# Two attention layers on one core: more split steps in the second layer, sums and outputs added by transfers, projections in half blocks

## The chip, the cores and the metric

The kernel runs on one core of a Trainium2 chip. The metric is the time of one execution on the device in microseconds. The engines are named as in the profile: PE is TensorE (PEld its weight loads), DVE is VectorE, ACT is ScalarE, POOL is GpSimd, SP issues most transfers.

## The reference

Two self-attention layers follow each other on x of 4 images with 4096 tokens of 256 channels, all in float32. Query and key have 32 channels; the second layer's values have 128.

```python
# layer 0
q, k, v = x @ Wq + bq, x @ Wk + bk, x @ Wv + bv          # 32, 32, 256 channels
attn = softmax(einsum('bnd,bmd->bnm', q, k), axis=-1)    # 4096 x 4096 per image
x = gamma * einsum('bnm,bmc->bnc', attn, v) + x
# layer 1
f, g, v = x @ Wf + bf, x @ Wg + bg, x @ Wh + bh          # 32, 32, 128 channels
beta = softmax(einsum('bqd,bkd->bqk', g, f), axis=-1)
x = x + einsum('bqk,bkd->bqd', beta, v) @ Wo + bo
```

## The kernel before

`fast_path` does all the work; `general_path` runs only when a flag, worked out at the end, says that values were out of range. The order is image by image, and in an image first layer, then second layer. A layer is cut into blocks of queries (first layer 16 blocks of 256, second layer 8 blocks of 512), and a block into **steps** over keys: 8 steps of 512 keys in the first layer, 16 steps of 256 keys in the second. There are 1024 steps in all, 128 for a layer of an image.

A step (`class Step`) has these parts:

- `scores`: TensorE multiplies keys and queries into the one score buffer `st` (128 x 1024, `ps_st` has one buffer), and ScalarE takes the exponential into `p`. The scores of step n + 2 are issued in the loop's turn for step n.
- In a **split** step the exponential is also taken with a small negative bias into `high`, rounded to the fast float32r form; VectorE makes `low` = p - high (`cut_low`) and `d` from low and high (`cut_both`). The values have three such parts too. The product is then three fast products (high, low and d, each with its part of the values), not one float32 product. All first-layer steps are split; in the second layer those with `i % 5 == 2`, three of 16 (2, 7, 12).
- `products_first`, `products_second`: TensorE adds the products into accumulators in PSUM. A whole second-layer step makes two float32 products of 512 columns, each two instructions in the profile; a split one makes six single ones.
- In the second layer VectorE also adds every step's p into `p_sum` (a copy for the first step, L696, then additions, L698), for the softmax's denominators.

Tiles come from pools with tags; tiles of one tag share its buffers, and a new one waits until an old one has been read. `wide` gives p three buffers (tag p), and high and p of a second-layer split step two (tag t); low and d share two (tag l).

After a block, `end_first` forms the new x: it writes it to DRAM (`x1_dram`), and x plus the second layer's bias to another DRAM tile (`x1_res`). `end_second` joins two accumulators and sums p_sum; its four output units multiply by Wo (L624), make the denominators (L625), and VectorE forms the result from PSUM and the reloaded x1_res (`load_old`, L605, L628), which SP writes to `out`.

Projections (`project_units`) of a block of 512 tokens are units too: transpose and split into parts, query and key projection with a store to DRAM (`qk_dram`), and values. POOL loads queries and keys back from DRAM, row by row (`load_q`, `load_k`). The next image's first-layer projections run beside this image's second layer, one block of tokens beside each block of queries; the second layer's run beside the first, the last of them in the second layer's first block. In image 0, three blocks are projected ahead of the first step, the other five within the first block.

The units are issued in the loop, after the scores of a later step and ahead of the step's products, paced evenly over the block's steps:

```python
        pace = NI[l] - (5 if l == 1 else 1)
        upto = min(len(units), -(-len(units) * (s.i + 1) // pace))
        todo = units[done:upto]
```

The Tile framework plans the final order of the instructions on each engine from this program order, with its own view of costs, and sets all waits. So an engine's order in the trace can differ from the written one; once planned it is fixed.

Of the kernel before, what the change touches and what calls it, by code (L numbers as in the profile page):

```python
# [61 lines left out]
EPS = 2.0**-12  # L63
AHEAD = 3

# [168 lines left out]
def fast_path(ctx: ExitStack, tc: tile.TileContext, x, w0, w1, wo, bo, gamma, out, off):  # L234
# [13 lines left out]
    split = [[l == 0 or i % 5 == 2 for i in range(NI[l])] for l in range(2)]  # L248
# [11 lines left out]
    def wide(tag, name, dtype=F32):  # L260
        return work.tile([P, 2 * QB], dtype, tag=tag, bufs={"d": 1, "p": 3}.get(tag, 2), name=name)
# [5 lines left out]
    def load_squares(key, tokens):  # L267

        turned[key] = []
        for c in range(NCC):  # L270
            t = work.tile([P, QB], F32, tag="squares", bufs=5, name=f"squares_{key[0]}_{key[1]}_{key[2]}_{c}")
            for a in range(P // S):
                ch = c * P + a * S
                nc.sync.dma_start(
                    t[a * S : (a + 1) * S, :].rearrange("j (b i) -> j b i", i=S),
                    tokens[:, ch : ch + S].rearrange("(b j) i -> j b i", j=S),
                )
            turned[key].append(t)

    def load_block(b, j):  # L280
        if b < B and j < NB:
            load_squares((b, 0, j), x[b, j * QB : (j + 1) * QB, :])


    x_nat = {}

    def load_first(j):
        if j < NB:
            x_nat[j] = []
            for n in range(j * NT, (j + 1) * NT):  # L290
                x_nat[j].append(data.tile([P, C], F32, tag="v1", bufs=V1, name=f"x_nat_{n}"))
                nc.sync.dma_start(x_nat[j][-1], x[0, n * P : (n + 1) * P, :])

    load_first(0)
    load_first(1)
# [8 lines left out]
    seen_v = const.tile([P, 2, B * NB, 2], F32, name="seen_v")  # L304
# [61 lines left out]
    xT, x_parts, k_t, v_t = {}, {}, {}, {}  # L366
    qk_dram, x1_dram, x1_res = {}, {}, {}
    q_t = {}


    def transpose_unit(b, l, j):
        def issue():
            xT[b, l, j] = data.tile([P, NCC, QB], F32, tag="xT", name=f"xT_{b}_{l}_{j}")
            for c in range(NCC):
                if b == l == 0:
                    ps = side_psum(f"psx_{j}_{c}")
                    for t in range(NT):
                        nc.tensor.transpose(ps[:, t * P : (t + 1) * P], x_nat[j][t][:, c * P : (c + 1) * P], ident)
                    nc.scalar.copy(xT[b, l, j][:, c, :], ps)
                else:  # L380
                    nc.vector.transpose(xT[b, l, j][:, c, :], turned[b, l, j][c])
            x_parts[b, l, j] = []
            for c in range(NCC):
                parts = [
                    work.tile([P, QB], F32R, tag="squares", bufs=5, name=f"x{what}_{b}_{l}_{j}_{c}") for what in "hl"
                ]
                nc.scalar.copy(parts[0], xT[b, l, j][:, c, :])  # L387
                nc.vector.tensor_sub(parts[1], xT[b, l, j][:, c, :], parts[0].bitcast(F32))  # L388
                x_parts[b, l, j].append(parts)
            if b == l == 0:  # L390
                load_first(j + 2)
            elif l == 0:
                load_block(b, j + 1)
            elif j == NB - 1:
                load_block(b + 1, 0)

        return issue

    def split_values(v, h, low, d, seen):
        nc.scalar.activation(h, v, AF.Copy, scale=1.0 - DOWN)  # L400
        nc.scalar.activation(low, v, AF.Abs, accum_out=seen)
        nc.vector.scalar_tensor_tensor(d, h.bitcast(F32), -1.0 - EPS, v, ALU.mult, ALU.add)
        nc.vector.scalar_tensor_tensor(low, d.bitcast(F32), 1.0 / EPS, h.bitcast(F32), ALU.mult, ALU.add)

    def project_units(b, l, j):
        key = (b, l, j)

        def qk_unit():
            ps = side_psum(f"psqk_{b}_{l}_{j}")
            for c in range(NCC):  # L410
                for n in range(2):
                    nc.tensor.matmul(  # L412
                        ps,
                        wqk[l][:, c, :],
                        x_parts[key][c][n],
                        start=(c == n == 0),
                        stop=(c == NCC - 1 and n == 1),
                    )
            whole = data.tile([2 * D, QB], F32, tag="qk", name=f"qk_{b}_{l}_{j}")
            parts = data.tile([P, QB], F32R, tag="qk_parts", name=f"qk_parts_{b}_{l}_{j}")  # L420
# [6 lines left out]
            qk_dram[key] = dram.tile([2, 2, D, QB], F32, name=f"qk_dram_{b}_{l}_{j}")  # L427
            nc.sync.dma_start(qk_dram[key].rearrange("h w d n -> (h w d) n"), parts.bitcast(F32))
            if b == l == 0:
                near = parts.rearrange("(h w d) n -> h w d n", h=2, w=2)  # L430
                load_k(b, l, j, near)
                if j == 0:
                    load_q(b, l, j, near)

        per = QB // CV[l]

        def v_unit(t0):
            def issue():
                ps = side_psum(f"psv_{b}_{l}_{j}_{t0}").rearrange("p (t c) -> p t c", c=CV[l])
                for t in range(per):  # L440
                    for c in range(NCC):
                        nc.tensor.matmul(  # L442
                            ps[:, t, :],
                            xT[key][:, c, (t0 + t) * P : (t0 + t + 1) * P],
                            wv[l][:, c, :],
                            start=(c == 0),
                            stop=(c == NCC - 1),
                        )
                tiles = slice(t0, t0 + per)
                seen = [seen_v[:, l, b * NB + j, n : n + 1] for n in range(2)]  # L450
                if l == 0:
                    split_values(ps, *(v0[j][what][:, tiles, :C] for what in ("h", "l", "d")), seen[t0 // per])
                    return
                for n in range(NT // G[1]):
                    i = j * NT // G[1] + n
                    v = ps[:, n * G[1] : (n + 1) * G[1], :]
                    if split[1][i]:
                        t = data.tile([P, 3, G[1], P], F32R, tag="v1_parts", bufs=sum(split[1]), name=f"v_{b}_{i}")
                        v_t[b, i] = {what: t[:, m] for m, what in enumerate(("h", "l", "d"))}
                        split_values(v, *v_t[b, i].values(), seen[n])  # L460
                    else:
                        v_t[b, i] = data.tile([P, G[1], P], F32, tag="v1", bufs=V1, name=f"v_{b}_{i}")
                        nc.scalar.copy(v_t[b, i], v)
                        nc.scalar.activation(v, v, AF.Abs, accum_out=seen[n])  # L464

            return issue

        return [transpose_unit(b, l, j), qk_unit] + [v_unit(t0) for t0 in range(0, NT, per)]

    def load_rows(dst, parts, which, halves):  # L470
        for n, h in enumerate(halves):
            nc.gpsimd.dma_start(dst[n * D : (n + 1) * D, :], parts[h, which])  # L472

    def load_q(b, l, j, parts=None):
        q_t[b, l, j] = data.tile([P, QB], F32R, tag="q", bufs=2, name=f"q_{b}_{l}_{j}")
        load_rows(q_t[b, l, j], qk_dram[b, l, j].bitcast(F32R) if parts is None else parts, 0, (0, 0, 1, 1))

    def load_k(b, l, j, parts=None):
        k_t[b, l, j] = data.tile([P, QB], F32R, tag="k", bufs=NB, name=f"k_{b}_{l}_{j}")
        load_rows(k_t[b, l, j], qk_dram[b, l, j].bitcast(F32R) if parts is None else parts, 1, (0, 1, 0, 1))  # L480
# [8 lines left out]
    class Step:  # L489
# [8 lines left out]
        def scores(self):  # L498
# [18 lines left out]
            nc.scalar.activation(self.p, s_flat, AF.Exp)  # L517

# [5 lines left out]
        def cut_both(self):  # L524
            if self.split:
                self.d = wide("d" if self.l == 0 else "l", f"d_{self.key}", F32R)
                nc.vector.scalar_tensor_tensor(  # L527
                    self.d, self.low.bitcast(F32), -1.0 / EPS, self.high.bitcast(F32), ALU.mult, ALU.add
                )

# [13 lines left out]
        def products_second(self, acc):  # L544
            v = v_t[self.b, self.i]
            some = [i for i in range(NI[1]) if split[1][i]]
            for p, v, which, first, last in (
                (
                    (self.high, v["h"], 0, self.i == some[0], False),
                    (self.low, v["l"], 0, False, self.i == some[-1]),  # L550
                    (self.d, v["d"], 1, self.first, self.last),
                )
                if self.split
                else ((self.p, v, 1, self.first, self.last),)
            ):
                for g in range(G[1]):
                    nc.tensor.matmul(  # L557
                        acc[which],
                        v[:, g, :],
# [6 lines left out]
    def end_first(b, j, acc):  # L566
# [11 lines left out]
        def residual(s):  # L578
            def issue():
# [6 lines left out]
                if part == 0 and s == 0:  # L586
                    x1_dram[b, jj] = dram.tile([QB, C], F32, name=f"x1_dram_{b}_{jj}")
                    x1_res[b, jj] = dram.tile([QB, C], F32, name=f"x1_res_{b}_{jj}")
# [53 lines left out]
    for j in range(AHEAD):  # L642
        run(project_units(0, 0, j))
# [153 lines left out]
```

## Time and profile before

| what | value |
|---|---|
| time, median of 3 runs (lowest, highest) | 3222.8 us (3222.76, 3225.62) |
| the profiled execution's own time | 3222.18 us |
| its span, first to last instruction | 3220.4 us |
| granted TensorE clock | 0.998 |
| PE, DVE, ACT, POOL busy | 3166.5, 2691.5, 1988.8, 661.3 us |
| DMA engines, hardware queue and software queue | 16.0%, 4.5% |
| first layer of image 0, 1, 2, 3 | 488.9, 451.9, 451.9, 451.9 us |
| second layer of image 0, 1, 2, 3 | 341.8, 343.5, 343.5, 322.7 us |

A row of the profile's groups gives the line, the engine, the operation, the tiles (out<-in), the shapes and the count, then busy time and the mean of one in ns, then the idle time of the engine ahead of these instructions and what ended it. The stage times are from the starts of the first score matmul (L505) of each stage in the timeline; the first image's first layer starts 24.2 us into the span, and the last figure goes to the end of the span.

### The profile page before, as it was taken

How to read it: one execution, taken by the hardware profiler on the slowest of the kernel's cores; microseconds unless marked ns; L12 is line 12 of the kernel's file. 1: busy time of each engine (PE TensorE's matmuls, PEld its weight loads, DVE VectorE, ACT ScalarE, POOL GpSimd, SP SyncE). 2: the span in 40 equal slices, each digit the busy share in tenths (PEclk: the TensorE clock that was granted, in tenths of full speed). 3: DMA queues.
4: the chain of work that ended last, by engine and by line, in shares of the span. 5: the costliest groups of instructions: out<-in, count | busy, mean ns of one | idle time of the engine just before them, and what ended most of it. 6: DMA issues, size and time to landing. Idle time of an engine off the chain costs nothing. (4 is left out here: it accounts for less than half of the span.)

```text
span 3220.4 us, 51144 instructions
## 1 busy us (share of the span) xinstructions
PE 3166.5 (98%) x19460; PEld 2613.0 (81%) x19460; DVE 2691.5 (84%) x3181; ACT 1988.8 (62%) x2483; POOL 661.3 (21%) x784
## 2 busy tenths in 40 slices
PE   8999999999999999999999999999999999999998
PEld 7999997566799999655679999966558999995554
DVE  7888888888888888788888888878888888887776
ACT  6666666655566666565556666655555666665554
POOL 3222223000232222200022222310002222241000
PEclk9999999999999999999999999999999999999999
DMA  4111123221212112322121112232222211121110
GB/s 120 47 47 44 50 50 83 56 53 49 59 44 54 44 52 49 79 53 53 49 64 42 49 50 50 61 70 52 51 52 57 53 41 47 46 70 47 36 36 31
DMA packets 368653, 172.16 MB, mean 53 GB/s; under 512 B 257392, under 2 KB 343664, under 8 KB 368400
## 3 DMA queue, kind: packets, MB, share of 16 engines
q1 hardware_dynamic: 342528, 134.29, 16.0%
q0 software_dynamic: 24960, 34.18, 4.5%
q8 instruction: 157, 2.57, 0.3%
q14 instruction: 96, 0.79, 0.1%
q10 hardware_dynamic: 912, 0.33, 0.0%
HBM read 99.22 MB, written 67.11 MB: 52 GB/s over the span
## 5 line engine op out<-in xcount | busy, mean ns | idle before, releaser
L517 ACT ACTIVATE p<-st 128x1024 f32<-128x1024 f32 x1024 | 1044.5, 1020 | 393.6 <-PE st L505 369.5
L515 ACT ACTIVATE high<-st,down 128x1024 fp32r<-128x1024 f32 x608 | 678.8, 1116 | 683.6 <-PE st L505 572.7
L527 DVE SCALAR_TENSOR_TENSOR d<-low,high 128x1024 fp32r<-128x1024 f32 x608 | 761.2, 1252 | 208.3 <-PE acc L536 202.9
L522 DVE TENSOR_TENSOR low<-p,high 128x1024 fp32r<-128x1024 f32 x608 | 810.6, 1333 | 134.2 <-ACT p L517 134.2
L557 PE MATMUL acc<-p,v 128*128 128x512 f32 x1664 | 795.2, 597 | 0.0
L505 PE MATMUL st<-q,k 128*128 128x256 f32 (+1 forms) x3072 | 778.6, 361 | 8.4 <-ACT p L517 8.3
L698 DVE TENSOR_TENSOR p_sum<-p_sum,p 128x1024 f32<-128x1024 f32 x480 | 587.1, 1223 | 60.7 <-ACT p L517 47.5
L505 PEld LDWEIGHTS st<-q,k 128*128 128x128 f32 x3072 | 461.2, 189 | 210.7 <-ACT p L517 113.3
L536 PE MATMUL acc<-v0d,d 128*128 128x258 f32 x4096 | 591.7, 284 | 1.7 <-DVE d L527 1.6
L536 PE MATMUL acc<-v0h,high 128*128 128x258 f32 x4096 | 588.6, 283 | 1.6 <-ACT high L515 1.6
L536 PE MATMUL acc<-v0l,low 128*128 128x258 f32 x4096 | 587.0, 283 | 0.5 <-DVE low L522 0.5
L536 PEld LDWEIGHTS acc<-v0d,d 128*128 128x128 f32 x4096 | 533.1, 189 | 6.7 <-DVE d L527 3.6
L536 PEld LDWEIGHTS acc<-v0h,high 128*128 128x128 f32 x4096 | 534.1, 190 | 3.4 <-ACT high L515 2.0
L536 PEld LDWEIGHTS acc<-v0l,low 128*128 128x128 f32 x4096 | 532.7, 189 | 0.8 <-DVE low L522 0.7
L557 PEld LDWEIGHTS acc<-p,v 128*128 128x128 f32 x1664 | 308.4, 190 | 214.3 <-issue 184.7
L593 POOL TENSOR_TENSOR x_res<-x,bo 128x256 f32<-128x256 f32 x128 | 216.3, 1690 | 889.9 <-DVE g L583 482.0
L472 POOL DMA_DIRECT2D q<-qk_dram x252 | 123.9, 501 | 1166.1 <-PE st L505 1143.0
L676 POOL TENSOR_TENSOR x_res<-x_res,bv 128x256 f32<-128x256 f32 x128 | 189.6, 1482 | 114.4 <-DMA x_res<-in_x 85.0
L442 PE MATMUL psv<-wv,xT 128*128 128x128 f32 (+1 forms) x1024 | 194.8, 331 | 6.8 <-DVE qk L423 6.1
L442 PEld LDWEIGHTS psv<-wv,xT 128*128 128x128 f32 x1024 | 159.6, 192 | 29.8 <-DVE qk L423 8.5
L472 POOL DMA_DIRECT2D k<-qk_dram x224 | 109.6, 500 | 245.2 <-PE st L505 140.3
L388 DVE TENSOR_TENSOR xl<-xT,xh 128x512 fp32r<-128x512 f32 x128 | 87.1, 683 | 5.1 <-ACT xh L387 4.7
(96 smaller groups left out, 1701.9 us busy)
## 6 DMA issues: line engine op xcount, KB each, us to landing
x_res<-in_x SPq DMA_DIRECT2D x128, 128.0 KB, 2.2
qk_dram<-qk_parts SPq DMA_DIRECT2D x64, 256.0 KB, 2.1
x_dram<-x SPq DMA_DIRECT2D x128, 128.0 KB, 1.7
x_res<-x_res SPq DMA_DIRECT2D x128, 128.0 KB, 1.7
squares<-x_dram SPq DMA_DIRECT2D x256, 64.0 KB, 2.3
x_old<-x_res SPq DMA_DIRECT2D x128, 128.0 KB, 2.0
out<-x_old SPq DMA_DIRECT2D x128, 128.0 KB, 1.7
q<-qk_dram POOLq DMA_DIRECT2D x252, 64.0 KB, 2.1
```

The costliest lines, as they stand in the source:

```text
L442: nc.tensor.matmul(ps[:, t, :], xT[key][:, c, (t0 + t) * P : (t0 + t + 1) * P], wv[l][:, c, :], start=(c == 0), stop=(c == NCC - 1),)
L472: nc.gpsimd.dma_start(dst[n * D : (n + 1) * D, :], parts[h, which])
L505: nc.tensor.matmul(st[:, g, :], k_t[b, l, kt // NT][:, kt % NT * P : (kt % NT + 1) * P], q_t[b, l, j * n // QB][:, q0 : q0 + n], start=Tru ...
L515: nc.scalar.activation(self.high, s_flat, AF.Exp, bias=down)
L517: nc.scalar.activation(self.p, s_flat, AF.Exp)
L522: nc.vector.tensor_sub(self.low, self.p, self.high.bitcast(F32))
L527: nc.vector.scalar_tensor_tensor(self.d, self.low.bitcast(F32), -1.0 / EPS, self.high.bitcast(F32), ALU.mult, ALU.add)
L536: nc.tensor.matmul(acc[2 * s + which][:, :W], p[:, g * QB0 + s * P : g * QB0 + (s + 1) * P], v0[self.i][v][:, g, :], start=self.first and ...
L557: nc.tensor.matmul(acc[which], v[:, g, :], p[:, g * QB : (g + 1) * QB], start=first and g == 0, stop=last and g == G[1] - 1,)
L593: nc.gpsimd.tensor_add(x_old[s], x_new[s], bo_sb)
L676: nc.gpsimd.tensor_add(x_res[b, j][t], x_res[b, j][t], bv)
L698: nc.vector.tensor_add(p_sum, p_sum, s.p)
```

## The change

There are four parts.

- The second layer's split steps are six of 16 (`SPLIT1`) instead of three.
- The exponentials of five of the whole steps (`MOVED_SUMS`) are not added by VectorE: POOL's queue copies the first into an SBUF tile (tag e, one buffer) and adds the other four to it with accumulating transfers. VectorE starts its own sum by adding the first two that remain, and `end_second` adds the moved sum.
- `end_first` writes x plus bias straight to `out`. The output unit scales its product on ScalarE into `y`, and POOL's queue adds y to `out` with an accumulating transfer. `x1_res` and `load_old` are gone.
- Projections are done in half blocks of 256 tokens, at steps named in a `plan`: the transpose, two steps (four in the first layer) later the query and key projection, one step later the values. In the second layer a half of the next image's starts every seven steps. In image 0's lead, odd halves use the buffers of tag v1_parts, so that two halves are under way. Square loads (transposing reads) are issued by half, when the half before has been projected.

The core of the diff:

```diff
+SPLIT1 = (1, 4, 6, 9, 11, 14)
+MOVED_SUMS = (0, 3, 7, 10, 13)
...
-    split = [[l == 0 or i % 5 == 2 for i in range(NI[l])] for l in range(2)]
+    NH = N // QB0
+    split = [[l == 0 or i in SPLIT1 for i in range(NI[l])] for l in range(2)]
...
             nc.scalar.activation(self.p, s_flat, AF.Exp)
+            if l == 1 and i in MOVED_SUMS:
+                if i == MOVED_SUMS[0]:
+                    moved_sums[b, j] = wide("e", f"p_sum_moved_{b}_{j}")
+                    nc.gpsimd.dma_start(moved_sums[b, j], self.p)
+                else:
+                    nc.gpsimd.dma_start(moved_sums[b, j], self.p, accum_op=ALU.add)
...
+        def add_up(self, p_sum):
+            if self.l == 0 or self.i in MOVED_SUMS:
+                return
+            kept = [i for i in range(NI[1]) if i not in MOVED_SUMS]
+            if self.i == kept[0]:
+                first_p.append(self.p)
+            elif self.i == kept[1]:
+                nc.vector.tensor_add(p_sum, first_p.pop(0), self.p)
+            else:
+                nc.vector.tensor_add(p_sum, p_sum, self.p)
...
-                nc.sync.dma_start(x1_res[b, jj][row : row + P, :], x_old[s])
+                nc.sync.dma_start(out[b, n * P - b * N : (n + 1) * P - b * N, :], x_old[s])
...
+        nc.vector.tensor_add(p_sum, p_sum, moved_sums[b, j])
         nc.vector.tensor_add(sums, p_sum[:, :QB], p_sum[:, QB:])
...
-                nc.vector.scalar_tensor_tensor(y[t], ps[:, :C], inverse[:, 1, n : n + 1], y[t], ALU.mult, ALU.add)
+                y = small(f"y_{key}_{t}")
+                nc.scalar.activation(y, ps[:, :C], AF.Copy, scale=inverse[:, 1, n : n + 1])
                 row = j * QB + t * P
-                nc.sync.dma_start(out[b, row : row + P, :], y[t])
+                nc.gpsimd.dma_start(out[b, row : row + P, :], y, accum_op=ALU.add)
...
+    lead = [project_units(0, 0, h) for h in range(2 * AHEAD)]
+    run([u[0] for u in lead[:2]])
+    for h in range(2 * AHEAD):
+        run(lead[h][1:])
+        run([u[0] for u in lead[h + 2 : h + 3]])
...
+    def plan(b, l, j, ends):
+        units = {}
+        def put(i, *some):
+            units.setdefault(i, []).extend(some)
+        if l == 0:
+            if j >= 2:
+                t, qk, v = project_units(b, 1, j - 2)
+                put(0, t), put(4, qk), put(5, v)
+            for n, u in enumerate(ends):
+                put(1 + n, u)
+            return units
+        if j == 0:
+            for n, u in enumerate(ends):
+                put(1 + n, u)
+            for n, h in enumerate((NH - 2, NH - 1)):
+                t, qk, v = project_units(b, 1, h)
+                put(6 * n, t), put(6 * n + 2, qk), put(6 * n + 3, v)
+        else:
+            for n, u in enumerate(ends):
+                put(1 + n, u)
+        if b + 1 < B:
+            for h in range(NH):
+                i = 12 + 7 * h - j * NI[1]
+                for n, u in zip((0, 2, 3), project_units(b + 1, 0, h)):
+                    if 0 <= i + n < NI[1]:
+                        put(i + n, u)
+        return units
```

The transpose unit for a half now makes one transpose and one pair of parts for both halves of the channels (128 x 512), as large as one of the two of a block before; the query and key projection has 256 columns instead of 512; a value unit has the same size as before in the first layer.

## The prediction

> **What bounds the kernel now.** I read the page first: engine shares, then the costliest groups, then the timeline of TensorE to find where each block of queries begins, last the waits and the timeline of ScalarE inside one block.
>
> ```profile
> PE 3166.5 (98%) x19460; PEld 2613.0 (81%) x19460; DVE 2691.5 (84%) x3181; ACT 1988.8 (62%) x2483; POOL 661.3 (21%) x784
> ...
> L517 ACT ACTIVATE p<-st 128x1024 f32<-128x1024 f32 x1024 | 1044.5, 1020 | 393.6 <-PE st L505 369.5
> L515 ACT ACTIVATE high<-st,down 128x1024 fp32r<-128x1024 f32 x608 | 678.8, 1116 | 683.6 <-PE st L505 572.7
> L527 DVE SCALAR_TENSOR_TENSOR d<-low,high 128x1024 fp32r<-128x1024 f32 x608 | 761.2, 1252 | 208.3 <-PE acc L536 202.9
> L522 DVE TENSOR_TENSOR low<-p,high 128x1024 fp32r<-128x1024 f32 x608 | 810.6, 1333 | 134.2 <-ACT p L517 134.2
> L557 PE MATMUL acc<-p,v 128*128 128x512 f32 x1664 | 795.2, 597 | 0.0
> ...
> L698 DVE TENSOR_TENSOR p_sum<-p_sum,p 128x1024 f32<-128x1024 f32 x480 | 587.1, 1223 | 60.7 <-ACT p L517 47.5
> ```
>
> TensorE is busy 98%, VectorE 84%. A matmul's mean (597 ns on L557) includes its pipeline; what counts is the spacing of issues in the timeline. There I read 0.43 us for each of the four instructions of a whole second-layer step, 0.215 us for one of the six in a split step and for a score matmul of 512 columns, 0.12 us for 256 or 258 columns. So a whole step costs TensorE 4 x 0.43 + 2 x 0.215 = 2.15 us, a split step 6 x 0.215 + 0.43 = 1.73, a first-layer step 24 x 0.12 + 4 x 0.12 = 3.35.
>
> The starts of the score matmuls give the stages. First-layer blocks take 27.0 without and 29.6 us with a projection, against 8 x 3.35 = 26.8 and 29.4 of issue: nothing to win. Second-layer blocks 2 to 7 of images 0 to 2 take 41.75 us (block 1: 40.4), the first block 52.6; in the last image, which projects nothing ahead, 37.2 and 45.0. Issue per block: 13 x 2.15 + 3 x 1.73 = 33.1, outputs 4 x 0.66 = 2.6, projection 20 x 0.215 = 4.3: 40.1 or, without projection, 35.8. So **1.4 to 1.7 us of each block is idle, and near 8 to 10 of the first**. The chain of exponentials shows how the idle time arises:
>
> ```profile
> 3021.11 1.11 ACT L515 ACTIVATE high<-st,down 128x1024 fp32r<-128x1024 f32 x1 [1.17 <-PE st L505]
> 3022.12 1.02 ACT L517 ACTIVATE p<-st 128x1024 f32<-128x1024 f32 x1
> 3023.94 1.02 ACT L517 ACTIVATE p<-st 128x1024 f32<-128x1024 f32 x1 [0.81 <-PE st L505]
> 3026.13 1.02 ACT L517 ACTIVATE p<-st 128x1024 f32<-128x1024 f32 x1 [1.16 <-PE st L505]
> ```
>
> There is one score buffer (ps_st), so scores, exponential and next scores alternate. At least 0.81 us passes between two exponentials; a whole step takes 1.02 + 0.83 = 1.85 us of this **chain**, a split one 2.03 + 0.81 = 2.84 (3021.11 to 3023.94). The block's chain is 13 x 1.85 + 3 x 2.84 = 32.6 us, below the issue; but after a split exponential TensorE runs out of placed work: 0.33 us three times a block in the timeline, and the rest is waits for VectorE:
>
> ```profile
> PE acc L557 <- DVE d L527: 13.7, 32, 1.5
> PE st L505 <- ACT p L517: 8.3, 10, 1.7
> PE psv L442 <- DVE qk L423: 6.1, 4, 1.8
> ```
>
> **What the Trainium skill says.** "DMA: Bandwidth & Descriptors", section "SWDGE vs HWDGE vs iDMA": only GpSimd's queue can accumulate during a transfer, so all additions land on POOL. The same page, "Rules for kernel authors": a transfer that adds into bytes must wait for the earlier one's semaphore, so the five of a block are serial. No run here shows either. Same page, "Anatomy of one DMA — SWDGE (gpsimd) path": a transfer costs about 2.0 us plus its bytes at 436 per ns; for POOL's 64 KB loads that is 2.15, the profile has 2.1. "TensorE: Matmul & The Clock Gate", section "Architectural detail: the array is 16× 32×32, not 1× 128×128": ScalarE and VectorE run strictly in order. The trace agrees: ScalarE stood 47.8 us, 49 times, behind its own cast waiting for VectorE (L424).
>
> **The change, part by part.**
>
> 1. *Three more split steps per second-layer block.* TensorE saves 3 x (4 x 0.43 - 6 x 0.215) = 1.29 us a block. ScalarE gets 3 x 1.01 us, and the chain grows by 3 x (2.84 - 1.85) to 35.5 us. VectorE gets 3 x (1.22 + 1.22) = 7.3 us (low, d), which the last four of the six products wait for. Steps 4, 6 and 9, 11 lie two apart and share the two buffers of tag t, so the high exponential of step 6 waits for the first products of step 4 (0.43 us more in the chain, twice); TensorE has step 5's products to do meanwhile.
>
> 2. *Five exponentials added by transfers.* VectorE loses a copy (0.75) and four additions (4 x 1.22), one addition becomes the first one's partner, and end_second adds one: 15 additions and a copy become 11 additions, 19.1 to 13.4 us, -5.7. POOL issues 5 x some 0.55 us (the row of its 128-partition weight loads). One transfer moves 512 KB: 2.0 + 1.2 = 3.2 us by the page if reading and adding the destination is free, 2.0 + 3 x 1.2 = 5.6 if each of its three passes costs the same; I take 5.6 (estimate), with 3.2 and 10 as ends. It holds its p buffer: three p buffers, reused five exponentials later, 2 x 2.84 + 2 x 1.85 + 0.8 = 10.2 us. Queued behind a waiting addition on POOL are q and k loads, not due for several steps.
>
> 3. *Outputs.* VectorE's 4 x 0.48 us become 4 x some 0.385 on ScalarE (row L613's size), 1.9 off VectorE. SP loses x1_res's reload (128 transfers, 2.0 us each, hidden: nothing). POOL gets 4 additions of 128 KB a block, 0.55 us of issue; y's four buffers are free until the next block, so 3 or 6 us of landing is hidden; if they serialised, the p additions behind them would be late.
>
> 4. *Half blocks.* Same multiplications; score projection 8 x 0.12 instead of 4 x 0.215 per block, +0.1 us. The transpose, the projection and the values now lie 2 and 1 steps apart instead of running at one pace, so the first block's waits on VectorE (6.1 us and idle ScalarE there) should mostly go. What is late next there: key block 7 is projected at step 8 and wanted by the scores placed at step 12, some 9 us later; four small steps on ScalarE and VectorE (2), the store (2.1) and POOL's four loads (4 x 0.5 + 2.1) take 8. I allow 2 us of idle for it. SP's square loads double in number at half size; it is not behind.
>
> VectorE's total per block with projection: 37.5 before, about 37.4 after (-5.7 + 7.3 - 1.9 + small), in a shorter block: 90% to 93%. That is where stalls return.
>
> Sum for an image with projection: issue is 8 x (33.1 + 2.6 + 4.3) + 2.6 = 323 of 343.5 us, idle 20. After: 323 - 10.3 + 0.9 = 314. Idle: twice as many split steps, each a 0.33 us wait, adds 1.0 a block; fewer additions beside them give some 0.2 back. I take 2.4 a block, plus 2 in the first: 21. So 335, **-8.5 an image, -25 for three**. Bounds: 1.6 and 3.2 a block. Last image: seven blocks 37.2 to 34.5 + 2.4 = 36.9, -2; first 45.0 to 34.5 + 2.6 + 2.4 + 2 = 41.5, -3.5. Start: 91.4 us to the end of block 0, with 26.8 + 8 x 5.2 = 68 of issue (a block's transposes 0.9, its projection 4.3) and 8 before the first value product (timeline); with two under way I take a third of the other 15, **-5** (0 to -10). First layer 0 (±4), tail 0: its additions are as many. Total -36: the profiled execution's 3222.2 us (span 3220.4, 1.8 around it; the runs' median is 3222.8) becomes **3186**.
>
> **Rivals.**
>
> *A larger gain.* The additions moved lie beside four of the six split steps, so VectorE is free when low and d are wanted, and idle stays 1.6 a block: 0.8 x 32 = 26 more, 3160. For it: d waits of 0.7 us with an addition between low and d. Against: the 0.33 waits are of the chain, not of VectorE.
>
> *The chain binds.* ScalarE's other work in a block (projections 5.4, y 1.5, o 0.8) fits the 0.81 gaps only by luck in time. Wholly unabsorbed: 35.5 + 7.7 = 43.2 us a block. From 78% unabsorbed it passes 41.5. Full price: 1.7 x 21 + 0.6 x 7 - 17 (first blocks, still shorter) - 5 (start) = +18, 3240; about three quarters: 3220. For it: the casts that block ScalarE double in number. Against: now projections add only 0.2 idle to a block.
>
> *The transfers bind (slower).* The five are serial, and the last must be read before the next block's first may write: 5 T must fit some 36 us, so from T = 7.2 us on, the p buffers come late and exponentials wait. Each us beyond costs 5 x 32 = 160 us; T = 8 gives about 3186 + 130 = 3310. For it: no row shows an adding transfer. Against: 5.6 estimated, DMA engines 20% busy.
>
> That the change doesn't do what it says: instructions are placed by a planner (the timeline has products ahead of earlier-written outputs), so split steps may be clustered; that is in the bounds of idle.
>
> **How the numbers follow.** Forecast 43% (3170 to 3203), larger gain 25% (3145 to 3170), chain 15% (3205 to 3240, a third each way), transfers 17%. The measurement tells 0.2%, 6.4 us, from no change. Faster 0.43 + 0.25 + 0.05 = 0.73, same 0.07, slower 0.20. Range 3148 to 3232, leaving out most of the transfers and the best of the gain.
>
> **What would show it.** Whole-step products 1280 instead of 1664, high 704 instead of 608; additions on VectorE 352 instead of 480; blocks at 36.9 (last image) and near 41; first block near 44. Step 2 is wrong if p exponentials wait for a transfer or additions land after over 7 us; step 1's idle if waits of L557 on d exceed 1 us a block; step 4 if the first block stays above 48. Over 3232 the forecast is wrong in mechanism, not size.

## The result and the profile after

The changed kernel takes **3232.1 us** (median of 11 runs, 3230.3 to 3233.2); the kernel before took 3224.0 us beside it. The ratio is **1.0026, 95% interval 1.0017 to 1.0034: slower by a quarter of a per cent**, where 1.1% faster was forecast.

First the page of the changed kernel: engine shares, the costliest groups (line engine op, out<-in, shapes, count, then busy us, mean ns, idle before and what ended it) and, from the DMA issues, KB and us to landing.

```profile
PE 3159.7 (98%) x19908; PEld 2653.3 (82%) x19908; DVE 2679.5 (83%) x3237; ACT 2146.8 (66%) x2835; POOL 898.9 (28%) x1108
...
L539 ACT ACTIVATE high<-st,down 128x1024 fp32r<-128x1024 f32 x704 | 786.2, 1117 | 734.5 <-PE st L529 532.8
L541 ACT ACTIVATE p<-st 128x1024 f32<-128x1024 f32 x1024 | 1045.8, 1021 | 230.8 <-PE st L529 225.3
L552 DVE TENSOR_TENSOR low<-p,high 128x1024 fp32r<-128x1024 f32 x704 | 937.5, 1332 | 192.4 <-ACT p L541 191.7
L557 DVE SCALAR_TENSOR_TENSOR d<-low,high 128x1024 fp32r<-128x1024 f32 x704 | 865.6, 1230 | 235.2 <-PE acc L577 232.3
...
L595 PE MATMUL acc<-p,v 128*128 128x512 f32 x1280 | 614.7, 594 | 0.0
...
L570 DVE TENSOR_TENSOR p_sum<-p_sum,p 128x1024 f32<-128x1024 f32 x288 | 350.3, 1216 | 8.2 <-ACT p L541 5.8
L547 POOL DMA_DIRECT2D p_sum_moved<-p x128 | 113.1, 884 | 527.0 <-ACT p L541 425.5
...
p_sum_moved<-p POOLq DMA_DIRECT2D x160, 512.0 KB, 4.6
...
out<-y POOLq DMA_DIRECT2D x128, 128.0 KB, 3.4
```

The counts are those that the change asks for: 1280 whole products, 704 high exponentials, additions on VectorE 288 here and 64 on two other lines. VectorE's total hardly moved (2691.5 to 2679.5 us), ScalarE's rose by 158 us. PE's share is 98% as before: with modelled ends, a page cannot show that TensorE now waits. The stage times can. They are read from the starts of the score matmuls in TensorE's timeline, in us:

| | before | after | forecast |
|---|---|---|---|
| start to the second layer of image 0 | 513.1 | 516.0 | about 508 |
| first layer, images 1 to 3 | 451.9 each | 453.2, 452.7, 451.8 | as before |
| second layer, images 0 to 2 | 341.8, 343.5, 343.5 | 338.2, 337.4, 338.2 | about 335 |
| its first block (images 1, 2) | 52.6 | 43.4, 44.0 | near 44 |
| its other blocks, mean (image 1) | 41.5 | 42.0 | near 41 |
| second layer of image 3, to the end of the span | 322.7 | 342.4 | about 317 |
| its blocks (3 to 7) | 37.2 | 39.2 | 36.9 |

The loss is in the last image, where nothing is projected: a block needs 1.3 us less of TensorE and takes 2.0 us more. ScalarE's timeline in one such block (start us, us, what, and in brackets the idle time before it and who ended it):

```profile
3019.58 1.11 ACT L539 ACTIVATE high<-st,down 128x1024 fp32r<-128x1024 f32 x1 [0.73 <-PE st L529]
3020.60 1.02 ACT L541 ACTIVATE p<-st 128x1024 f32<-128x1024 f32 x1
...
3022.43 1.02 ACT L541 ACTIVATE p<-st 128x1024 f32<-128x1024 f32 x1 [0.45 <-PE st L529]
3023.35 0.47 ACT L664 ACTIVATE y<-pso,inverse 128x256 f32<-128x256 f32 x1
3025.32 1.12 ACT L539 ACTIVATE high<-st,down 128x1024 fp32r<-128x1024 f32 x1 [1.50 <-PE st L529]
3026.38 1.03 ACT L541 ACTIVATE p<-st 128x1024 f32<-128x1024 f32 x1
3027.30 0.47 ACT L664 ACTIVATE y<-pso,inverse 128x256 f32<-128x256 f32 x1
3028.62 1.02 ACT L541 ACTIVATE p<-st 128x1024 f32<-128x1024 f32 x1 [0.85 <-PE st L529]
```

From a split step's first exponential to the next step's it takes 2.85 us (3019.58 to 3022.43), once, with an output's scaling in between, 3.30 (3025.32 to 3028.62); where the planned order has four whole-product instructions and an output unit ahead of the next scores, even a whole step takes 2.89 (3022.43 to 3025.32), where its least is 1.85. The chain of a block is 10 x 1.85 + 6 x 2.84 = 35.5 us at best, and 39.2 as it runs; TensorE's issue is 34.5. Over the whole kernel TensorE waited for d and for p in the chain, and ScalarE's high waited for its buffer (engine, what waited, for what: us, times, longest):

```profile
PE acc L595 <- DVE d L557: 23.6, 40, 1.5
PE st L529 <- ACT p L541: 6.6, 18, 1.1
```

```profile
ACT high L539 <- DVE p_sum L570: 12.8, 9, 1.6
ACT high L539 <- PE acc L595: 10.7, 7, 1.7
ACT high L539 <- DVE d L557: 10.2, 8, 3.0
```

The last three lines have no counterpart before. The first two, 23.5 us, are step 6's and 11's high, which want the buffer that step 4's and 9's still hold; 22 us of them lie in images 0 to 2. The third, 10.2 us, lies in the first layers, most of it some 8 us after their start.

In one block of the last image (3010.0 to 3049.2 us) the profile counts this for TensorE:

```profile
PE acc L595 <- DVE d L557: 1.2, 2, 0.8
PE st L529 <- ACT p L541: 0.2, 1, 0.2
```

With each instruction given its issue time (0.43 or 0.215 us, an output unit 0.66) and followed from start to start, TensorE is idle for 4.8 us in each of blocks 3 to 7: 2.7 ahead of products with d and 1.4 ahead of scores. In the kernel before it was 1.5: 0.7 and 0.4. So most of the loss shows as standing for d. Whether d is late by VectorE's load, by its own path, or because late scores leave TensorE no other products meanwhile, this trace alone does not tell.

### The profile page after: what moved, and what is told of

Its sections match the earlier page's. It is cut to its first block, busy times and chain, and to the rows that moved or that the text cites. A ratio compares the mean times of both kernels' runs of the same rounds, so it can differ in the third digit from the quotient of the medians.

```text
span 3230.1 us, 54167 instructions
## 1 busy us (share of the span) xinstructions
PE 3159.7 (98%) x19908; PEld 2653.3 (82%) x19908; DVE 2679.5 (83%) x3237; ACT 2146.8 (66%) x2835; POOL 898.9 (28%) x1108
## 4 chain that ended last, share of the span: by engine, by line
PE 83%; DVE 6%; issue 4%; ACT 4%; DMA 2%; SPq 1%; POOL 0%; DVEq 0%; ACTq 0%; POOLq 0%
PE acc L577 44%; PE acc L595 18%; PE st L529 13%; PE psv L463 4%; DVE d L557 2%; DVE low L552 2%; ACT p L541 2%; PE psqk L421 2%; PE pso L658 1%; ACT high L539 1%; DMA squares<-x_dram 1%; SPq L279 1%; DMA squares<-in_x 1%; PE pso L659 0%; DMA p_sum_moved<-p 0%
## 5 line engine op out<-in xcount | busy, mean ns | idle before, releaser
L539 ACT ACTIVATE high<-st,down 128x1024 fp32r<-128x1024 f32 x704 | 786.2, 1117 | 734.5 <-PE st L529 532.8
L552 DVE TENSOR_TENSOR low<-p,high 128x1024 fp32r<-128x1024 f32 x704 | 937.5, 1332 | 192.4 <-ACT p L541 191.7
L557 DVE SCALAR_TENSOR_TENSOR d<-low,high 128x1024 fp32r<-128x1024 f32 x704 | 865.6, 1230 | 235.2 <-PE acc L577 232.3
L529 PE MATMUL st<-q,k 128*128 128x256 f32 (+1 forms) x3072 | 742.9, 349 | 10.0 <-ACT p L541 6.6
L595 PE MATMUL acc<-p,v 128*128 128x512 f32 x1280 | 614.7, 594 | 0.0
L634 POOL TENSOR_TENSOR x_res<-x,bo 128x256 f32<-128x256 f32 x128 | 198.7, 1552 | 877.8 <-DVE x L623 877.7
L595 PEld LDWEIGHTS acc<-p,v 128*128 128x128 f32 x1280 | 236.3, 189 | 148.8 <-issue 123.2
L570 DVE TENSOR_TENSOR p_sum<-p_sum,p 128x1024 f32<-128x1024 f32 x288 | 350.3, 1216 | 8.2 <-ACT p L541 5.8
L547 POOL DMA_DIRECT2D p_sum_moved<-p x128 | 113.1, 884 | 527.0 <-ACT p L541 425.5
L463 PEld LDWEIGHTS psv<-wv,xT 128*128 128x128 f32 x1024 | 158.4, 191 | 32.6 <-issue 14.6
L666 POOL DMA_DIRECT2D out<-y x128 | 116.7, 930 | 243.0 <-ACT y L664 220.1
```

The costliest lines, as they stand in the source:

```text
L463: nc.tensor.matmul(ps[:, t, :], xT[key][:, c, t * P : (t + 1) * P], wv[l][:, c, :], start=(c == 0), stop=(c == NCC - 1),)
L529: nc.tensor.matmul(st[:, g, :], k_t[b, l, kt // NT][:, kt % NT * P : (kt % NT + 1) * P], q_t[b, l, j * n // QB][:, q0 : q0 + n], start=Tru ...
L539: nc.scalar.activation(self.high, s_flat, AF.Exp, bias=down)
L552: nc.vector.tensor_sub(self.low, self.p, self.high.bitcast(F32))
L557: nc.vector.scalar_tensor_tensor(self.d, self.low.bitcast(F32), -UP, self.high.bitcast(F32), ALU.mult, ALU.add)
L570: nc.vector.tensor_add(p_sum, p_sum, self.p)
```

## The experiments

Three theories stood: the **chain** (one score buffer for scores and exponentials), **VectorE** (low and d come late), and the **transfers** (the moved sums hold p or POOL's queue). All kernels are variants of the changed one unless said otherwise; medians, with the ratio to the kernel before and its 95% interval. Every edit is planned anew, so a difference between two runs holds the difference of their orders too.

| run | us | ratio |
|---|---|---|
| half blocks alone | 3193.5 | 0.9905 [0.9888, 0.9921] |
| + new outputs | 3195.8 | 0.9918 [0.9901, 0.9934] |
| + moved sums | 3204.3 | 0.9942 [0.9925, 0.9959] |
| + one more split step | 3211.2 | 0.9961 [0.9947, 0.9976] |
| + two more split steps, six in all: the change | 3232.1 | 1.0026 [1.0017, 1.0034] |
| the change, high copied from p | 3181.5 | 0.9870 [0.9854, 0.9889] |
| the change, high copied from p, old outputs | 3178.6 | 0.9861 [0.9845, 0.9878] |

### Three split steps instead of six

```diff
-SPLIT1 = (1, 4, 6, 9, 11, 14)
+SPLIT1 = (1, 6, 11)
```

(The buffers of v1_parts are set to five, and five halves are loaded at the start as before.)

> The changed kernel with three split steps (1, 6, 11) instead of six; moved additions, outputs and half blocks stay. Chain theory (one score buffer, scores and exponentials alternate, a split step costs 2.84 us of it against 1.85): the last image's second-layer blocks go from 39.2 back to about 37.2 us, the others to about 41, total near 3205. VectorE theory (low and d come late): also shorter, but the waits for d would go too, near 3205; this run alone does not tell these two apart. Transfer theory (the five adding transfers hold the p buffers or the queue): blocks stay at 39 and more, total 3230 or above, since TensorE gets its 41 us back.

Measured: 3204.3 us, blocks of the last image 37.3. So the three more split steps, which save 41 us of issue on TensorE, cost 28 us. Chain and VectorE both allow that.

### All sums on VectorE

```diff
-MOVED_SUMS = (0, 3, 7, 10, 13)
+MOVED_SUMS = ()
...
-        nc.vector.tensor_add(p_sum, p_sum, moved_sums[b, j])
```

> The changed kernel with all sums added by VectorE as before, no moved sums; six split steps stay. Chain theory: the last image's blocks stay near 39 to 39.5, total 3225 to 3245. VectorE theory: 5.7 us more work on VectorE a block makes it clearly slower, blocks 41 and 44, total above 3280. Transfer theory: faster, blocks near 37, total below 3200.

Measured: 3242.5 us, ratio 1.0060 [1.0044, 1.0077], last image's blocks 39.3. With 5.7 us more on VectorE the blocks of the last image are as long as with the moved sums. TensorE's idle time ahead of products with d stays as well (2.6 us a block, 2.7 in the changed kernel). VectorE's load does not bind there, and on balance the transfers cost nothing there; over the whole kernel they are worth 10 us.

### High copied from p

```diff
-                self.high = wide("t", f"high_{self.key}", F32R)
-                nc.scalar.activation(self.high, s_flat, AF.Exp, bias=down)
             self.p = wide("t" if self.split and l == 1 else "p", f"p_{self.key}")
             nc.scalar.activation(self.p, s_flat, AF.Exp)
+            if self.split and l == 1:
+                self.high = wide("t", f"high_{self.key}", F32R)
+                nc.scalar.activation(self.high, self.p, AF.Copy, scale=1.0 - DOWN)
```

(The first layer keeps its order.) The bias is -2^-13, so the scaled copy is the same number but for rounding.

> The changed kernel where second-layer split steps take p first and then high as a scaled copy of p from SBUF on ScalarE, so that the score buffer is free after 1.02 us instead of 2.03 while ScalarE's work stays. Chain theory: the chain shrinks by up to 6 x 0.8 us a block; blocks 36 to 37 in the last image (39.2 now), near 40 in the others (41.9 now), total 3150 to 3180. VectorE theory: low and d come as late or later, no gain, 3225 to 3245. Transfer theory: no change.

Measured: **3181.5 us**, 1.5 over the chain theory's range; last image's blocks 36.1, blocks 2 to 8 of image 1 40.9 on average (42.0 before the edit). ScalarE's timeline in the last image:

```profile
2996.73 1.02 ACT L541 ACTIVATE p<-st 128x1024 f32<-128x1024 f32 x1 [0.83 <-PE st L529]
2997.78 1.06 ACT L544 ACTIVATE high<-p 128x1024 fp32r<-128x1024 f32 x1
2998.91 1.02 ACT L541 ACTIVATE p<-st 128x1024 f32<-128x1024 f32 x1
3001.09 1.03 ACT L541 ACTIVATE p<-st 128x1024 f32<-128x1024 f32 x1 [1.16 <-PE st L529]
3002.15 1.06 ACT L544 ACTIVATE high<-p 128x1024 fp32r<-128x1024 f32 x1
3003.11 1.01 ACT L541 ACTIVATE p<-st 128x1024 f32<-128x1024 f32 x1
```

The copy takes as long as the exponential did (1.06 us), but the next scores are made under it: p follows high with no gap, and a split step takes 2.18 (2996.73 to 2998.91) and 2.02 us instead of 2.84. ScalarE's work is nearly unchanged, VectorE's too: what differs is the score buffer's time, and the order of p and high. TensorE's idle time ahead of products with d falls from 2.7 to 0.4 us in a block of the last image, though the path from scores to d (p, high, low, d) is no shorter: it was late scores that left TensorE standing for d.

### Control: p first, both from the score buffer

```diff
             self.p = wide("t" if self.split and l == 1 else "p", f"p_{self.key}")
             nc.scalar.activation(self.p, s_flat, AF.Exp)
             if self.split:
                 self.high = wide("t", f"high_{self.key}", F32R)
                 nc.scalar.activation(self.high, s_flat, AF.Exp, bias=down)
```

(The order that results in the second layer, not the edit line by line; the first layer keeps its order.)

> The changed kernel with p taken before high in the second layer's split steps, both still from the score buffer. A control for the run in which high is copied from p: p comes 1 us earlier here too, but the score buffer is held for 2.03 us as before. Chain theory: no gain, last image's blocks 38.5 to 40, total 3222 to 3242. If the gain of the copy came from p's earlier time (VectorE's additions start sooner) or from another order of the buffers of tag t: blocks near 36 to 37, total 3180 to 3195.

Measured: 3211.7 us, ratio 0.9963 [0.9949, 0.9977]; the last image's blocks 38.3. I had expected no gain; 20 of the 51 us of the run before come with the order alone (the last image's blocks fall from 39.2 to 38.3). What is left for the score buffer's early release is 30 us, and 17.5 of these lie in the last image's second layer (336.3 to 318.8 us). With this order the waits of high for products and p_sum are gone, and what remains is this line, of which 8.3 us lie in the first layers:

```profile
ACT high L542 <- DVE d L560: 10.0, 9, 2.5
```

TensorE's waits for d (L595 in the changed kernel, 23.6 us) fall to 3.9 us too, so the 20 us are not put down to one cause. With the copy these waits are 3.6 us, hardly less: the 30 us do not come from them.

### Three buffers for high and p of split steps

```diff
-        return work.tile([P, 2 * QB], dtype, tag=tag, bufs={"d": 1, "e": 1, "p": 3}.get(tag, 2), name=name)
+        return work.tile([P, 2 * QB], dtype, tag=tag, bufs={"d": 1, "e": 1, "p": 3, "t": 3}.get(tag, 2), name=name)
```

(On the kernel with all sums on VectorE, whose missing tile makes room.)

> The changed kernel without moved sums (3242 us) and with three buffers instead of two for tag t, which holds high and p of the second layer's split steps; the tile of the moved sums makes the room. Hold theory (high of steps 6 and 11 waits until the products and d of steps 4 and 9 have released its buffer, which stretches the chain of exponentials): 3222 to 3234, and ScalarE's waits for products, d and p_sum ahead of high, 41 us in the run with two buffers, fall below 20. If the hold costs nothing beside the chain: 3238 to 3246.

Measured: 3221.6 us, ratio 0.9995 [0.9986, 1.0003], against 3242.5 with two buffers: **the hold costs 21 us**. They come from images 0 to 2, whose second layers fall from 341 to 335 us; the last image's blocks stay at 39.1 (39.3 with two). In the second layers, where these waits of high for products, d and p_sum came to 40 us with two buffers, none is left. (This trace puts 420.6 us of ScalarE's waits ahead of high to no releaser, but all of them lie in the first layers.) Hold and chain are thus two costs, in different places. In the changed kernel the hold's waits in the second layers are 23.5 us, not 40, and no run takes them away alone.

### The same copy in the kernel before

The edit is that of "High copied from p", made in the kernel before.

> The kernel before with only that edit (p first, high copied from p in the second layer's three split steps). Chain theory: at most the 0.33 us after each of three split exponentials, 96 places, comes back: 3195 to 3215. VectorE and transfer theories: no change, 3220 to 3226.

Measured: 3226.1 us, ratio 1.0007 [0.9998, 1.0016]; blocks 42.2 and 37.0. The chain theory's number was wrong: with three split steps the chain (32.6 us) lies under the issue (35.8), and giving it room returns nothing. The 0.33 us gaps that I had read as its cost are not the chain's: in the last image's blocks TensorE's idle time ahead of products with d falls from 0.7 to 0.1 us, and ahead of scores it rises from 0.4 to 0.8. That the planned order makes these gaps is likely, but not shown.

### Four split steps

```diff
-SPLIT1 = (1, 4, 6, 9, 11, 14)
+SPLIT1 = (1, 6, 11, 14)
```

(The buffers of v1_parts as in the run with three.)

> The changed kernel with four split steps (1, 6, 11, 14), all else as changed. Chain theory: issue is 35.3 us and the chain 33.5 for a block of the last image, so blocks 37 to 37.6, total 3200 to 3212, between three split steps (3204) and six (3232), with the rise coming only after four. A cost in proportion to the number of split steps would give 3213.6.

Measured: 3211.2 us; the last image's blocks 37.65. The total is inside the chain's range but within 3 us of a proportional cost, and one first block of 45.7 us stood behind late keys, so it decides nothing. The blocks alone go 37.3, 37.65, 39.2 with three, four and six: the rise comes mostly after four, as a chain that overtakes the issue would have it.

### High copied from p, no moved sums

The edits of "High copied from p" and "All sums on VectorE" together.

> High copied from p, six split steps, and no moved sums: VectorE adds all. Chain theory: with the chain no longer in the way VectorE's 5.7 us a block are worth more than the 10 us that they were worth in the changed kernel: last image's blocks 37 to 38.5 instead of 36.1, the others 42 or more, total 3205 to 3240. If VectorE does not bind even then: within 10 us of 3181.

Measured: 3201.0 us, ratio 0.9934 [0.9917, 0.9950]; last image's blocks 36.7, the others 41.3 (image 1), so the total lies below the range expected and above the other (within 10 us of 3181). The moved sums are worth 19.6 us here, more than the 10 in the changed kernel; but the blocks grow by only 0.4 to 0.6 us for 5.7 us of VectorE's work, so VectorE still has some room.

### Half blocks with the new outputs

The edits of "Three split steps" and "All sums on VectorE" together.

> Half blocks and the outputs added by transfers alone: three split steps (1, 6, 11), no moved sums. If the gain of 20 us with three split steps is the half blocks' (first block of the second layer 40 us instead of 52.6): 3200 to 3212. If the moved sums carry it: 3215 to 3225.

Measured: 3195.8 us, faster than either range. Against 3204.3 with moved sums: **with three split steps the transfers cost 8.5 us**. In the trace with moved sums TensorE stands for late keys, once 3.4 us in the first block of the last image's second layer; POOL issued their loads 5.7 us after SP had issued their store (2900.16 to 2905.87), against 2.3 us without moved sums (2896.74 to 2898.99):

```profile
PE st L529 <- DMA k<-qk_dram: 5.2, 2, 3.4
```

ScalarE there also waits for transfers that hold p, 10.3 us in 6 places. Neither is among the changed kernel's waits.

### Outputs as before

The diff's lines for outputs are undone: x1_res, load_old, the result formed by VectorE, SP's store.

> The changed kernel with the outputs as before (reload of x plus bias, VectorE forms the result, SP stores); six split steps and moved sums stay. Chain theory: four scalings of 0.47 us leave ScalarE, where they fall into the chain: last image's blocks 38 to 38.8 instead of 39.2, and the end of the span, 5 us longer after the change, comes back in part: 3205 to 3225. If VectorE's 1.9 us a block count for more: 3235 to 3260.

> High copied from p (3181 us) and the outputs as before. With the score buffer free early ScalarE has time for the scalings: within 6 us of 3181, of which 3 to 5 less for the end of the span. If VectorE is the next bound: 3188 to 3200.

> Half blocks alone: three split steps (1, 6, 11), no moved sums, outputs as before. If the half blocks carry the gain of 27 us of the run with half blocks and new outputs: 3190 to 3202. If the new outputs carry a third or more of it: 3203 to 3215.

Measured: with six split steps and the chain as changed 3236.1, ratio 1.0043 [1.0026, 1.0059], last image's blocks 39.2: the scalings do not lengthen the chain by what I had said, and the old outputs are 4 us slower here, in the range that I had given for VectorE's 1.9 us. With high copied from p 3178.6, not to be told from 3181.5. Half blocks alone 3193.5: they carry the gain (in this run units follow the new plan and the split steps are 1, 6, 11 instead of 2, 7, 12; neither was tried by itself). The new outputs change the time by between -4 and +3 us. The span's longer end is theirs only in part: with old outputs and high copied from p it stays 25 us (61.4 us for the last block and the end against 36.2 for a block). But in the changed kernel the last test of values (L732 before, L788 after) stands for an output's adding transfer, since its tile takes the buffer of a y:

```profile
3209.72 0.28 DVE L732 TENSOR_SCALAR good<-inverse 128x256 f32<-128x256 f32 x1
3216.42 0.29 DVE L788 TENSOR_SCALAR good<-inverse 128x256 f32<-128x256 f32 x1 [2.05 <-DMA out<-y]
```

## Why the prediction was wrong

**Part 1, the split steps, failed in three of its terms.** The first and largest is the idle time: "each a 0.33 us wait, adds 1.0 a block ... I take 2.4", with 3.2 as the bound; in the last image idle was 39.2 - 34.5 = 4.7 us a block. I had worked out the chain at 35.5 us and had it above the issue (34.5) in that image, and still added up idle as if issue were the bound. A block can't be shorter than its longest chain plus what the planned order misses. Over the larger of chain and issue the last image's blocks run 1.4 us before, 1.5 with three split steps, 2.3 with four and 3.7 with six, but 1.6 where high is copied: the miss was larger where chain and issue lay close. That alone is 2.3 x 7 = 16 of the 46 us between forecast and result. "TensorE has step 5's products to do meanwhile" was the second: without moved sums the shared buffers of steps 4, 6 and 9, 11 cost 21 us, though TensorE had work, because the wait sits in the chain and not on TensorE. Third, the 0.33 us itself: the copy in the kernel before showed that those gaps were not the chain's.

**The rival that came true is "the chain binds"**, given 15% and 3205 to 3240. Its mechanism is shown by the copy and its control. Its place was wrong: I priced it at 1.7 us a block in images 0 to 2 and 0.6 in the last, by ScalarE's other work; it came to 0.5 and 2.0 us. That the total still lies in its range is luck.

**Part 2, the moved sums: right on the transfers' time**, 4.6 us from issue to landing against 5.6 estimated and 7.2 as the point from which they bind, with 0.88 us of issue on POOL against 0.55. That they were worth only 10 us was not said anywhere: I had used VectorE's 93% as a reason for stalls. Waits of products for d came to 23.6 us in 32 blocks, 0.7 a block, under the 1 us that I had named as the limit: that sign missed a failure that was there, since the profile counts only part of TensorE's idle time.

**Part 3, outputs: right but for the end of the span.** ScalarE needs 0.47 us for y and not 0.385, which does not show in the time; the landing of an adding transfer, taken as hidden, costs 2.05 us in the tail.

**Part 4, half blocks: right in mechanism, wrong for the start.** The first block went from 52.6 to 43.4 us, as forecast (near 44); in that of image 1 TensorE's waits for VectorE fell from 3.6 to 1.9 us. Half blocks alone gain 29 us. The start was forecast at -5 us and came out at +2 (block 0 ended 93.4 us into the span, 91.4 before): two halves under way brought nothing there. The end of the span, forecast at 0, is 5 us longer (63.3 - 39.3 = 24.0 us beyond a block's period, before 56.1 - 37.2 = 18.9). Part of it is step 14's split: its last products wait 1.5 us for d in the tail, where nothing else is left to do (0.3 before). Another part is the 2.05 us for an output's transfer. But half blocks alone, with neither of the two, already end 3.5 us later than before (22.4 us), so these parts do not simply add up, and the rest is not settled.

In sum the gap of 46 us is 25 in the last image's second layer (of it some 18 in blocks 2 to 8, 2 in the first block, 5 at the end), some 10 in the other second layers, 8 up to the second layer of image 0, and 2 in the later first layers.

Of the forecast's signs the counts, the first block, the transfer time and the waits for d held; two failed (36.9 for the last image's blocks: 39.2; near 41 for the others: 42.0).

## What to carry to other kernels

Before work is taken off the busiest engine, add up the longest chain through a single buffer (here scores, exponential, next scores), with the gaps that the trace shows between its links; if the change brings it near the engine's own sum, the time will be the larger of the two plus a margin, which was 4 to 10 per cent in the last image's blocks here. When two results are made from one scarce buffer whose chain is the longest, let the second be made from the first, so that the buffer is free after one; where the chain was shorter than the issue, this gained nothing. Steps that hold a buffer pair should not lie closer than the pair is held.

## What the runs showed that I had not expected

- Copying 128x1024 numbers from SBUF with a scale takes ScalarE 1.06 us, hardly less than the exponential from PSUM (1.12 with rounding to float32r): the 30 us between copy and control came from when the score buffer was free, not from ScalarE's time.
- An adding transfer of 512 KB within SBUF took 4.6 us to land, where a plain copy of the same size took 2.9; one of 128 KB into DRAM took 3.4 us, where a plain store from SP takes 1.7.
- The same five moved additions cost 8.5 us with three split steps and gained 10 and 20 us with six: on a planned order a part's worth depends on what else is late.
